# A two-layer decoder: the first two groups become single pairs of batches, the second a few steps behind the first

## The chip, the cores and the metric

The kernel runs on one core of a Trainium2 chip. The metric is the device time of one execution in microseconds. The core has five engines that run side by side, each working through its own queue in order: TensorE (PE, matrix products and transposes, with a separate row PEld for loading its stationary operand), VectorE (DVE), ScalarE (ACT), GpSimd (POOL) and SyncE (SP), which here issues all DMA transfers.

## The reference

Two decoder layers over 32 batches of 56 tokens with 128 features. Every batch has a memory of 1500 rows (`ctx_1024`). All of it is float32. Cut to what matters:

```python
x = LN(x + L0_attn(x))        # 16 heads of 8, window of 32
x = LN(x + L0_xattn(ctx, x))  # one head of 128 over 1500 memory rows
x = LN(x + L0_ffn(x))         # 8 experts of 512 (gelu), top 2
x = LN(x + L1_attn(x))        # gated recurrent mixer: tanh projections and a scan over tokens
x = LN(x + L1_xattn(x, ctx))  # 16 heads of 64 over 1500 memory rows
x = LN(x + L1_ffn(x))         # 1 shared + 8 routed experts of 256 (silu), top 2
```

The experts are computed densely: every token goes through every expert, and the mixing weights are zero for all but two. So an expert's weights are loaded once for each group of tokens that passes.

## The kernel before

**Groups.** The 32 batches form 16 pairs of two (112 tokens, `TP`) and 8 groups of two pairs (224 tokens, `T`). For a group there are three kinds of work:

- `pre`: self-attention, cross attention of layer 0, its experts, the recurrent mixer, and the queries for the cross attention of layer 1, folded with the keys' weights (`m1`). The cross attention of layer 0 also transposes each batch's memory and stores it in HBM as `memT`.
- `attention`: the cross attention of layer 1, with 896 query rows (16 heads of 56 tokens) against 1500 memory rows for each batch. It runs batch by batch in two blocks of 512 and 384 query rows. `load_attended` (L1050) brings a batch's memory into `amN`, `load_attended_T` (L1053) its transposed form into `amT`. The scores lie in two large buffers with the tags `s512` and `s384`.
- `post`: the output projection and the experts of layer 1.

**Order of the work.** Each kind of work is a Python generator, and a `Thread` steps it from one `yield` to the next. A `yield` gives the time that the thread should stay away, in a count of modelled TensorE time. The main loop steps `attention` and, after each step, the `pre` of the next group and the `post` of the last one, as far as they are due: `pre` is spread so that it ends at 88% of its group's attention, with `PRE_US` = 74 and `POST_US` = 31 as their modelled sizes. The order in which instructions are written down is a priority: a scheduler at build time places them in the engines' queues when it reckons their inputs and buffers are there, so that DMA loads with nothing to wait for go out far ahead of their place in the code.

**The opening.** Before the first score of `attention` there has to be a first group with its queries. The kernel opens with groups 0 and 1 together, four pairs:

```python
starts = [Thread(opening_a(0)), Thread(opening_a(1), aside)]
...
together(*starts, folding, lag=10)
load_attended_T(0)
together(Thread(opening_b()))
together(Thread(opening_c(0)), Thread(opening_c(1), aside))
```

`opening_a` is the self-attention and the cross attention of one group, each with its two pairs one after the other; `opening_b` sends both groups through the experts of layer 0 on one load of the weights; `opening_c` is the mixer, and for group 0 the queries. Group 1 uses other places than group 0 (`aside`): it keeps its tiles inside the buffers that attention uses later (`s512`, `s384`, the query buffer `qo[2]`, a tile `m`), reads memory into `amN` instead of `cxN`, and takes its PSUM banks from the pool `p_s` (three banks, tag `s`) instead of `p_f` (two banks, tag `f`). In the profile its tiles bear these names: `s<-qo,wu` is group 1's `f<-xT,wu`. `folding` multiplies the head weights of layer 1 (`in_heads_dram`) into `m1` and `n1`. `together` steps its threads in turn.

**Lines to know.** L142 and L151 are the helpers for every matmul and every transpose, so these are told apart by tiles. `load_x0` (L481) loads the memory of a pair, two DMAs. L507 stores `memT`. L642 and L644 load an expert's `wu` and `wd` (256 KB each, four buffers). L681 is the gelu, L705 adds an expert's output to `acc`. L809 copies queries into `qo`, of which there are three, one for a pair. L345 is the last step of a normalization. L998 copies scores out of PSUM.

Of the kernel before, what the change touches and what calls it, by code (L numbers as in the profile page):

```python
# [15 lines left out]
G = 4  # L16
NG = B // G
T = G * S
NJ = G // 2
TP = 2 * S  # L20
H0, DH0, WIN = 16, 8, 32
# [38 lines left out]
PRE_US, POST_US = 74.0, 31.0  # L60
# [4 lines left out]
def decoder_kernel(  # L65
# [232 lines left out]
    def wide_tile(tag, bufs=1):  # L298
        return work.tile([P, T], F32, tag=tag, name=tag, bufs=bufs)

# [61 lines left out]
    def ahead(a, b, tag="res"):  # L362
        r = tok_tile(tag)
        nc.gpsimd.tensor_tensor(r, a, b, ALU.add)
        return r
# [12 lines left out]
    def self_attention(xs):  # L378
        xT = to_features(xs, "xT")
        res = [ahead(t, obias) for t in xs]  # L380
        yield HOP
        qT, kT, oT = wide_tile("qT0"), wide_tile("kT0"), wide_tile("oT0")
        affine(qT, linear(sqw("wq0"), xT, T), vcol("bq0"))
        yield 0
        affine(kT, linear(sqw("wk0"), xT, T), vcol("bk0"))
        yield 0
        vs, kbs = [], []
        for j in range(NJ):
# [21 lines left out]
        for j in range(NJ):  # L410
# [59 lines left out]
        for j in range(NJ):  # L470
            ys.append(normalize(plus(linear(pair(oT, j), sqw("wo0"), D, TP), res[j]), "y"))
            yield 0
# [4 lines left out]
    def load_x0(p, g):  # L477
        cxN = contexts_0()
        for i in range(2):
            b = g * G + 2 * p + i  # L480
            nc.sync.dma_start(cxN[i][:, :, :D], mem[b].rearrange("(p c) d -> p c d", p=PK))  # L481

    def cross_attention_0(xs, g):
        cxN, qpad = contexts_0(), here(qpad0, "qpad")
# [3 lines left out]
        qp, oT, vT = wide_tile("qT0"), wide_tile("oT0"), wide_tile("kT0")  # L488
        affine(qp, linear(sqw("xq0"), xT, T), vcol("xbq0"))
# [3 lines left out]
            linear(sqw("xk0"), qp, T).rearrange("p (b s) -> p b s", b=G),  # L493
# [3 lines left out]
        for p in range(NJ):  # L497
            cxT = [big_tile(i) for i in range(2)]
            for i in range(2):
# [7 lines left out]
                nc.sync.dma_start(memT[g * G + 2 * p + i], cxT[i][:, : CK * PK])  # L507
# [48 lines left out]
            if p + 1 < NJ:  # L556
                load_x0(p + 1, g)
            elif g == 1:
                load_attended(0)
            elif max(g + 1, 2) < NG:  # L560
                load_x0(0, max(g + 1, 2))
# [7 lines left out]
            yield LOAD if p + 1 < NJ else HOP  # L569
        affine(vT, linear(sqw("xv0"), oT, T), vcol("xbv0"))  # L570
        yield HOP
        ys = []
        for j in range(NJ):
            ys.append(normalize(plus(linear(pair(vT, j), sqw("xo0"), D, TP), res[j]), "y"))
            yield 0
# [60 lines left out]
    def experts_0(groups):  # L636

# [9 lines left out]
        def each():  # L647
            for k in range(len(groups)):
                place["aside"] = aside if k else None
                yield k  # L650
            place["aside"] = None

        ws = weights(0)
        xT, w, acc, hT = {}, {}, {}, {}
        for k in each():
            xT[k] = to_features(groups[k], "xT")
        yield HOP
        for k in each():
            lg = tiny.tile([TP, NJ, E], F32, tag="lg", name="lg", bufs=2)
            nc.vector.tensor_copy(lg, router(xT[k], C_R0))  # L660
            picks = top2(lg)
            p1 = tiny.tile([TP, NJ], F32, tag="p1", name="p1", bufs=2)
            p2 = tiny.tile([TP, NJ], F32, tag="p2", name="p2", bufs=2)
            nc.vector.tensor_tensor(p2, picks[1][0], picks[0][0], ALU.subtract)
            nc.scalar.activation(p2, p2, AF.Exp)
            nc.vector.tensor_scalar_add(p1, p2, 1.0)
            nc.vector.reciprocal(p1, p1)
            nc.vector.tensor_tensor(p2, p2, p1, ALU.mult)
            w[k] = mix(picks, (p1, p2))
        yield 0  # L670
        for e in range(E + 1):
            last = (ws, dict(hT))
            if e < E:
                if e > 0:
                    ws = nxt
                if e + 1 < E:
                    nxt = weights(e + 1)
                for k in each():
                    hT[k] = hidden_tile()
                    for u in range(nu):  # L680
                        nc.scalar.activation(  # L681
                            hT[k][:, u, :],
                            linear(ws[0][:, u * D : (u + 1) * D], xT[k], T), AF.Gelu,
                            bias=vec[:, C_BUP + e * nu + u : C_BUP + e * nu + u + 1],
                        )
                        if len(groups) == 1:
                            yield 0
                yield 0
            for k in each():
                if e == 0:  # L690

                    wT = work.tile([E, T], F32, tag="wT", name="wT", bufs=1)
                    ps = bank(p_f, "f")
                    for j in range(NJ):
                        mm(pair(ps[:E], j), w[k][:, j, :], ident[:TP, :TP])
                    nc.vector.tensor_copy(wT, ps[:E, :T])
                    if len(groups) == 1:
                        yield HOP
                    acc[k] = [
                        plus(linear(pair(wT, j), bdn, D, TP), groups[k][j], "acc")  # L700
                        for j in range(NJ)
                    ]
                else:
                    for j in range(NJ):
                        nc.vector.scalar_tensor_tensor(  # L705
                            acc[k][j], down(last[1][k], last[0][1], nu, j),
                            w[k][:, j, e - 1 : e], acc[k][j], ALU.mult, ALU.add,
                        )
                        if len(groups) == 1:
                            yield 0  # L710
        both = []
        for k in each():
            both.append([normalize_twice(a, "y") for a in acc[k]])
        yield NORM
        return both


    def recurrent_mixer(both):
        hp = here(hp0, "hp")
        res, hs = [], [h for _, h in both]  # L720
        for t, _ in both:
            r = tok_tile("res")
            nc.vector.scalar_tensor_tensor(r, t, 2.0, rowb("bout1"), ALU.mult, ALU.add)
            res.append(r)
        affine(
            hp[:, :, 1 : S + 1], transposed(hs).rearrange("p (b s) -> p b s", b=G),
            vcol("lnb1"), vcol("lng1"),
        )
        mT = wide_tile("xT")
        m3 = mT.rearrange("p (b s) -> p b s", b=G)  # L730
# [11 lines left out]
        def state_in(c0, scale, bias, i):  # L742
            t = small[:, i * T : (i + 1) * T]
            nc.scalar.activation(
                t, linear(sq[:, c0 : c0 + SD], mT, T, SD), AF.Tanh, bias=bias[:, i : i + 1],
# [10 lines left out]
        u, g = wide_tile("kT0"), wide_tile("qT0")  # L756
        nc.scalar.activation(u, linear(sqw("wi1"), mT, T), AF.Tanh, bias=vcol("bi1"))

        new = small[:, 3 * T : 4 * T]
# [4 lines left out]
        nc.vector.memset(dec.rearrange("p (b s) -> p b s", b=G)[:, :, 0:1], 0.0)  # L764
# [4 lines left out]
        nc.scalar.activation(g, linear(sqw("wg1"), mT, T), AF.Tanh, bias=hbg, scale=0.5)  # L769
        yield 2.5  # L770

        z = wide_tile("oT0")
        nc.vector.scalar_tensor_tensor(
            z, linear(hwso, sta, T), vcol("bso1"), u, ALU.add, ALU.subtract
# [5 lines left out]
        for j in range(NJ):  # L780
# [10 lines left out]
    def query_input(both, g):  # L791
        res1[g] = [ahead(t, gbias, f"res1{g % 2}") for t, _ in both]
        hs = [h for _, h in both]
        xT = wide_tile("xT")
# [3 lines left out]
    def queries_1(xT, g):  # L798
        while not projected(2 * g - 2):
            yield None  # L800
        for i in range(H1 // 2):
            ps = bank(p_f, "f")
            for k in range(2):
                mm(ps[:, k * T : (k + 1) * T], m1[:, 2 * i + k, :], xT)
            src = ps[:, : 2 * T].rearrange("p (h b s) -> p b h s", h=2, b=G)
            for j in range(NJ):
                dst = qo[(2 * g + j) % 3][:, :, 2 * i * S : (2 * i + 2) * S]
# [89 lines left out]
    def load_x(g):  # L897
        xs = []
        for j in range(NJ):
            t = tok_tile("xin", 4)  # L900
            nc.sync.dma_start(t, x[g * T + j * TP : g * T + (j + 1) * TP, :])
            xs.append(t)
# [3 lines left out]

    def pre(g):
        if g == 1:
            yield from queries_1(query_input(both.pop(1), 1), 1)
            return  # L910
        xs = xin.pop(g) if g in xin else load_x(g)
# [4 lines left out]
        (xs,) = yield from experts_0([xs])  # L916
        xs = yield from recurrent_mixer(xs)
        xT = query_input(xs, g)
        yield HOP
        yield from queries_1(xT, g)  # L920


    first, both = {}, {}

    def opening_a(g):
        xs = load_x(g)
        load_x0(0, g)
        yield 0
        xs = yield from self_attention(xs)
        first[g] = yield from cross_attention_0(xs, g)  # L930

    def opening_b():
        both[0], both[1] = yield from experts_0([first[0], first[1]])

    def opening_c(g):
        both[g] = yield from recurrent_mixer(both[g])
        if g == 0:
            xT = query_input(both.pop(0), 0)
            yield HOP
            yield from queries_1(xT, 0)  # L940
# [3 lines left out]
    def post(g):  # L944
        xs, t0 = [], g * T
        for j in range(NJ):
            pp = 2 * g + j
# [4 lines left out]
            for h in range(H1):  # L952
# [12 lines left out]
                r, ps[:TP, :D], tgate[:TP], res1[g][j], ALU.mult, ALU.add  # L965
# [333 lines left out]
```

## Time and profile before

| | us |
|---|---|
| median of three runs | 2382.88 |
| lowest and highest | 2378.03, 2383.84 |
| the profiled execution | 2383.31 |
| its span, first to last instruction | 2381.6 |
| PE busy | 2247.1 (94%) |
| DVE busy | 1427.0 (60%) |
| ACT busy | 1262.7 (53%) |
| POOL busy | 254.3 (11%) |

The page gives busy times of each engine over the span and in 40 slices of it, in tenths. A timeline row has the start, the duration, the engine, the line, the operation and what it writes and reads (`out<-in`), a count where like instructions are merged, and in brackets the idle time ahead of it with what ended it. A float32 matmul shows as two instructions. Matmuls are pipelined, so that the distance from start to start, the pitch, tells what they cost in a dense stretch, and the mean duration does not. `PEclk` is the share of full speed that TensorE's clock was granted.

### The profile page before, as it was taken

The numbers are of one execution on the slowest core, as the hardware profiler recorded it, in microseconds if no ns is written. First come the engines' busy times: TensorE is split into PE (matmuls) and PEld (weight loads), VectorE is DVE, ScalarE is ACT, GpSimd is POOL, SyncE is SP. The second block draws the span as 40 slices with busy tenths as digits, with TensorE's granted clock in tenths as the row PEclk, the third lists the DMA queues.
The fourth block names the chain that finished last, engine by engine and source line by source line (L and its number), as shares of the span: only waits on it lengthen the run. The fifth ranks groups of instructions, "written<-read, shape, count | busy, mean of one in ns | idle before, by whom it ended". The sixth has DMA issues, their size and how long they took to land. (4 is left out here: it accounts for less than half of the span.)

```text
span 2381.6 us, 37426 instructions
## 1 busy us (share of the span) xinstructions
PE 2247.1 (94%) x14906; PEld 1769.6 (74%) x14906; DVE 1427.0 (60%) x2755; ACT 1262.7 (53%) x2212; POOL 254.3 (11%) x416
## 2 busy tenths in 40 slices
PE   6769799999999999999999999999999999999997
PEld 4548477767876779767887787777787678878787
DVE  3422566766576664766557665666647665566664
ACT  1324365555655456555565556554655555655542
POOL 3100200110021000220003100220002200020000
PEclk8878899999999999999999999999999999999998
DMA  5233010114320233113221133201331022210212
GB/s 157 79 113 91 11 40 26 29 54 122 93 66 16 66 102 108 47 29 108 85 82 37 53 103 94 72 27 59 111 97 58 27 91 62 71 42 28 80 34 82
DMA packets 158159, 163.81 MB, mean 69 GB/s; under 512 B 7417, under 2 KB 134817, under 8 KB 157857
## 3 DMA queue, kind: packets, MB, share of 16 engines
q1 hardware_dynamic: 157984, 161.42, 22.1%
q8 instruction: 118, 1.93, 0.3%
q14 instruction: 57, 0.46, 0.1%
HBM read 135.90 MB, written 25.49 MB: 68 GB/s over the span
## 5 line engine op out<-in xcount | busy, mean ns | idle before, releaser
L142 PE MATMUL v<-amN,s 125*128 125x129 f32 x5376 | 701.3, 276 | 1.8 <-ACT s L1086 1.8
L142 PEld LDWEIGHTS v<-amN,s 125*128 125x128 f32 x5376 | 663.2, 192 | 45.9 <-issue 29.7
L142 PE MATMUL s<-qo,amT 128*125 128x512 f32 (+1 forms) x1536 | 651.5, 547 | 4.7 <-ACT s L998 4.4
L998 ACT COPY s<-s 125x512 f32<-125x512 f32 (+1 forms) x768 | 396.6, 538 | 188.2 <-PE s L142 186.9
L1083 DVE TENSOR_TENSOR s<-s,nb 125x1536 f32<-125x1536 f32 (+1 forms) x256 | 394.3, 1557 | 108.9 <-ACT nb L1075 108.8
L142 PEld LDWEIGHTS s<-qo,amT 128*125 128x125 f32 x1536 | 264.0, 188 | 190.5 <-issue 114.9
L1086 ACT ACTIVATE s<-s 125x1536 f32<-125x1536 f32 (+1 forms) x256 | 337.6, 1327 | 91.3 <-DVE s L1083 87.1
L1001 DVE TENSOR_TENSOR m<-m,s 125x1024 f32<-125x1024 f32 (+1 forms) x256 | 279.0, 1090 | 70.4 <-ACT s L998 65.7
L342 POOL TENSOR_SCALAR rs<-mv 112x1 f32<-112x1 f32 x116 | 46.0, 396 | 1797.9 <-DVE mv L336 1598.8
L1103 ACT ACTIVATE ao<-v,rz 128x128 f32<-128x128 f32 x224 | 80.2, 361 | 176.7 <-DVE rz L1101 174.3
L681 ACT ACTIVATE hT<-f,vec 128x224 f32<-128x224 f32 x224 | 95.3, 449 | 96.8 <-PE f L142 95.1
L142 PE MATMUL f<-xT,wu 128*128 128x224 f32 x448 | 124.2, 381 | 2.8 <-DMA wu<-in_wup_dram 2.0
L142 PE MATMUL f<-pxT,w 128*128 128x224 f32 (+1 forms) x576 | 118.2, 343 | 2.1 <-DMA w<-in_gate_dram 1.3
L1001 DVE TENSOR_TENSOR m<-s 125x1024 f32<-125x1024 f32 x64 | 69.7, 1090 | 83.5 <-ACT s L998 83.2
L142 PEld LDWEIGHTS f<-wd,hT 128*112 128x112 f32 x896 | 104.7, 178 | 13.4 <-ACT hT L681 5.1
L705 DVE SCALAR_TENSOR_TENSOR acc<-f,wmix,acc 112x128 f32<-112x128 f32 x112 | 39.2, 350 | 125.8 <-PE f L142 125.8
L142 PE MATMUL f<-wd,hT 128*112 128x128 f32 x896 | 113.3, 275 | 0.0
L1075 ACT COPY nb<-t 125x512 f32<-125x512 f32 x64 | 34.0, 532 | 148.3 <-PE t L142 148.1
L142 PEld LDWEIGHTS f<-pxT,w 128*128 128x128 f32 x576 | 99.4, 195 | 15.3 <-issue 3.2
L142 PEld LDWEIGHTS f<-xT,wu 128*128 128x128 f32 x448 | 74.0, 194 | 21.2 <-ACT hT L681 7.4
L142 PEld LDWEIGHTS f<-w,h 128*112 128x112 f32 x512 | 67.6, 178 | 24.0 <-issue 9.2
L142 PE MATMUL f<-w,h 128*112 128x128 f32 x512 | 79.7, 279 | 2.0 <-DVE th L870 1.9
(313 smaller groups left out, 2694.2 us busy)
## 6 DMA issues: line engine op xcount, KB each, us to landing
amN<-in_mem_dram SPq DMA_DIRECT2D x36, 750.0 KB
amT<-memT SPq DMA_DIRECT2D x32, 750.0 KB, 4.4
cxN<-in_mem_dram SPq DMA_DIRECT2D x28, 750.0 KB
memT<-big SPq DMA_DIRECT2D x28, 750.0 KB, 5.0
wu<-in_wup_dram SPq DMA_DIRECT2D x56, 256.0 KB, 2.8
wd<-in_wdn_dram SPq DMA_DIRECT2D x56, 256.0 KB, 2.7
w<-in_gate_dram SPq DMA_DIRECT2D x72, 128.0 KB, 2.3
w<-in_up_dram SPq DMA_DIRECT2D x72, 128.0 KB, 2.5
```

The source lines that it names most:

```text
L142: nc.tensor.matmul(ps, lhsT=lhsT, rhs=rhs, start=start, stop=stop)
L342: nc.gpsimd.tensor_scalar(rs, mv[:, 1:2], mul, add, ALU.mult, ALU.add)
L681: nc.scalar.activation(hT[k][:, u, :], linear(ws[0][:, u * D : (u + 1) * D], xT[k], T), AF.Gelu, bias=vec[:, C_BUP + e * nu + u : C_BUP + ...
L705: nc.vector.scalar_tensor_tensor(acc[k][j], down(last[1][k], last[0][1], nu, j), w[k][:, j, e - 1 : e], acc[k][j], ALU.mult, ALU.add,)
L998: nc.scalar.copy(s[:, c, :], ps[:PK, :n])
L1001: nc.vector.tensor_tensor(m, a, s[:, c - 1 : c + 1, :], ALU.max)
L1075: nc.scalar.copy(nb, ps[:PK, :n])
L1083: nc.vector.tensor_tensor(c, c, nb.unsqueeze(1).to_broadcast([PK, 3, n]), ALU.add)
L1086: nc.scalar.activation(c, c, AF.Exp)
L1103: nc.scalar.activation(o, po[:, :D], AF.Copy, scale=rz)
```

## The change

The groups get different sizes: pair 0 alone, pair 1 alone, and then seven groups of two pairs.

- The helpers of `pre` take the number of pairs from their input. `experts_0` works on one group and returns `acc` before its normalization.
- `opening(0)`, the leader, goes from the self-attention to the queries with pair 0. `opening(1)`, the follower, starts six steps later with pair 1 in the places aside. It waits for the leader to have written down all its experts, goes through the experts with its own loads of the weights, and copies its `acc` out of the places aside by GpSimd once the leader is through. The head folding starts at step 12.
- The mixer and the queries of pair 1 are now `pre(1)`, stepped beside attention without a limit; then comes the `pre` of pairs 2 and 3, spread over the attention of pairs 0 and 1, and so on. There are now seven `pre` of two pairs beside attention; there were six.
- `load_x0` for pair 2 and `load_x` for its group are written down after the opening. `load_attended(0)` follows the follower's cross attention, `load_attended_T(0)` the leader's.
- The main loop paces by the attention time over all pairs (`PAIR_US` = 82.7) instead of from the start of each group; `post` keeps its pairs and its pacing. A `yield NORM` is added in the mixer.

```diff
-G = 4
-NG = B // G
...
+GROUPS = [[0], [1]] + [[p, p + 1] for p in range(2, NPAIR, 2)]
+NG = len(GROUPS)
...
     def pre(g):
         if g == 1:
-            yield from queries_1(query_input(both.pop(1), 1), 1)
+            yield from behind_experts(early.pop("acc"), 1)
             return
...
-    def opening_a(g):
+    def opening(g):
         xs = load_x(g)
-        load_x0(0, g)
+        load_x0(GROUPS[g][0])
         yield 0
         xs = yield from self_attention(xs)
-        first[g] = yield from cross_attention_0(xs, g)
...
+        xs = yield from cross_attention_0(xs, g)
         if g == 0:
...
+            load_attended_T(0)
+            acc = yield from experts_0(xs)
+            early["weights"] = True
+            yield from behind_experts(acc, g)
+            return
+        load_attended(0)
+        while "weights" not in early:
+            yield None
+        acc = yield from experts_0(xs)
+
+        while not leader.over:
+            yield None
+        place["aside"] = None
+        early["acc"] = []
+        for a in acc:
+            t = tok_tile("acc")
+            nc.gpsimd.tensor_copy(t, a)
+            early["acc"].append(t)
...
-    together(*starts, folding, lag=10)
-    load_attended_T(0)
-    together(Thread(opening_b()))
-    together(Thread(opening_c(0)), Thread(opening_c(1), aside))
+    n = 0
+    while not (leader.over and follower.over):
+        for t, at in ((leader, 0), (folding, 12), (follower, 6)):
+            if n >= at and not t.over:
+                t.step()
+        n += 1
+    load_x0(GROUPS[2][0])
+    xin[2] = load_x(2)
...
+        at = main.spent / PAIR_US
+        g = next((g for g in range(1, NG) if not pres[g].over), None)
+        if g == 1:
+            until(pres[1], 1e9)
+        elif g is not None:
+            since = 0 if g == 2 else GROUPS[g - 1][0]
+            part = (at - since) / (GROUPS[g][0] - since)
+            until(pres[g], PRE_US * part / 0.88)
```

## The prediction

> **What bounds the kernel now.** I read the page's slices first, then the span cut into stages, then the timelines of TensorE and of SP's queue. The page:
>
> ```profile
> PE   6769799999999999999999999999999999999997
> ...
> PEclk8878899999999999999999999999999999999998
> ```
>
> Of forty slices of 59.5 us, only the first five (and the last) are not full. The same, cut where the work changes:
>
> ```profile
> 8.00:77.00 69.00, 53.82 (x437) 38.28 (x438) 30.42 (x53) 17.97 (x36) 20.53 (x27) 0.80 0.39 119
> 77.00:113.00 36.00, 27.98 (x213) 21.13 (x213) 14.42 (x39) 14.44 (x28) 4.78 (x12) 0.86 0.30 111
> 113.00:145.00 32.00, 13.90 (x50) 8.94 (x51) 2.31 (x4) 3.67 (x7) 0.00 (x0) 0.60 0.46 140
> 145.00:174.00 29.00, 22.00 (x164) 15.82 (x162) 11.91 (x33) 11.70 (x21) 2.54 (x8) 0.85 0.24 85
> 174.00:200.00 26.00, 23.15 (x90) 17.73 (x91) 8.22 (x50) 9.70 (x20) 0.42 (x1) 0.61 0.43 114
> 200.00:241.00 41.00, 41.00 (x301) 39.54 (x301) 8.69 (x25) 18.76 (x48) 0.00 (x0) 1.00 0.24 73
> 241.00:276.20 35.20, 19.77 (x84) 13.66 (x83) 20.52 (x73) 7.24 (x18) 14.61 (x38) 0.71 0.05 14
> 276.20:435.60 159.40, 156.65 (x890) 116.99 (x889) 103.12 (x120) 99.41 (x165) 0.00 (x0) 1.00 0.10 30
> 435.60:2113.10 1677.50, 1634.22 (x11047) 1286.28 (x11047) 1058.74 (x2024) 954.72 (x1655) 196.94 (x286) 0.99 0.23 70
> 2113.10:2381.60 268.50, 253.88 (x1643) 210.77 (x1642) 168.32 (x336) 123.57 (x215) 9.24 (x16) 0.98 0.18 53
> ```
>
> Columns: stretch, length, then busy PE, PEld, DVE, ACT, POOL, granted clock, DMA share, GB/s. From 276.2 us, where the first score matmul of the big attention starts, PE is busy 97 to 98% at clock 1.00: there every matmul costs its pitch, and nothing else counts. The 276.2 us ahead of it are latency and DMA, with a clock down to 0.60. So a piece of work is dear in the opening and cheap behind it. The change moves work across this border.
>
> What one pair of batches waits for in the opening stands in SP's queue:
>
> ```profile
> 28.48 8.00 SPq L1165 DMA_DIRECT2D s<-in_heads_dram  x1
> ...
> 109.53 7.02 SPq L481 DMA_DIRECT2D cxN<-in_mem_dram  x2
> 116.64 15.40 SPq L481 DMA_DIRECT2D amN<-in_mem_dram  x2
> ...
> 163.50 6.81 SPq L481 DMA_DIRECT2D cxN<-in_mem_dram  x2
> 170.41 16.28 SPq L1050 DMA_DIRECT2D amN<-in_mem_dram  x2
> 186.79 7.95 SPq L642 DMA_DIRECT2D wu<-in_wup_dram  x1
> ```
>
> Four loads of a batch's memory take 34 us (109.5 to the last one's first use at 143.7, at about 100 GB/s), and PE stands for them in 113 to 145. At 163.5 the same four loads go out again for later work, and the expert weights wu queue behind them: issued at 186.79, in use at 199.79.
>
> **The change, part by part.** Let X be the moment of the first score matmul, 276.2 now. The sum is X, plus 2105.4 (2381.6 - 276.2), plus what moves behind X.
>
> *Work that moves behind X.* Pairs 2 and 3 lose their joint opening and become an ordinary `pre`. Its price: groups 1 to 6 take 1677.5 / 6 = 279.6 us each, made of attention, one `pre` and one `post`. Attention alone shows between two reloads of amT in the first group:
>
> ```profile
> 298.03 0.33 SPq L1053 DMA_DIRECT2D amT<-memT  x1
> ...
> 343.53 0.34 SPq L1053 DMA_DIRECT2D amT<-memT  x1
> ...
> 385.01 0.34 SPq L1053 DMA_DIRECT2D amT<-memT  x1
> ```
>
> It is 41.5 us (nothing beside it) to 45.5 us (with some queries) a batch, 43 taken: 172 for four. 107.6 remain for `pre` and `post`; the kernel's own weights 74 : 31 split them into 75.8 and 31.8. Bounds: 41.5 gives 80, 45.5 gives 69; I take 76. Window 0 had no `pre` and now has one, as windows 1 to 6 do; DVE 63% and ACT 57% busy there leave them room, so PE's pitch is the price. Its DMAs go along: four memory loads, four stores of memT and sixteen loads of weights lift the DMA share of window 0 from 0.10 to the 0.23 of the others, which hides them there.
>
> *Pair 1* now does its mixer and queries beside attention. Queries: 32 matmul instructions of 112 columns. Their pitch, from this row (32 in 3.56 us to the next start):
>
> ```profile
> 495.63 3.72 PE L142 MATMUL f<-qo,n 128*128 128x112 f32 x32
> 499.19 1.07 PE L142 MATMUL v<-amN,s 125*128 125x129 f32 x8
> ```
>
> 0.111 us each, 3.6 us; some 20 more for the mixer at 0.11, 2 us. Out goes what window 0 did for group 1: 32 of 224 columns at 0.19, 6.1 us. Net -0.5. The mixer's long chain (241 to 269 in the trace) hides under attention, which needs pair 1 only a pair later; uncovered it would cost its 28 us. The extra `yield NORM` and the new pacing are emission only: each `pre` still has to be through at 88% of its window, 0. The GpSimd copy of acc is one of 0.5 us, and attention's first score tile waits for it, since the follower's work lies in the buffers s512 and s384.
>
> *X, stage by stage.* (1) Self-attention: the first pair's oT is written at 52.64, the second's at 75.44; the second goes, and with it one of two normalizations: xT of the cross attention comes at 83.07 now, about 57 then (52.6 + 4.7 for one tile, reading the same chain). The wait for `heads1`, in use at 45.85, stays: PE takes it in order. (2) The first cross pair runs from 83.07 until cxN is free at 109.53, 26.4 us, with both groups in step. The leader is six steps ahead, which I count as 4 us: cxN free at 57 + 26.4 - 4 = 80 (75 if the head folding lies behind the leader's chain, 84 if it gets nothing from its lead). (3) The second cross pair, its four loads and the wait (113 to 167) go. (4) The experts. The loads at L481 for the next group and at L1050 for batches 0 and 1 are free to go out at 80, ahead of wu of expert 2, whose buffer is only freed by expert 0. If they do, as at 163.5, the distance 163.50 to 199.79 = 36.3 us repeats: expert 2 starts at 116. (5) From there 6 experts of the leader and 8 of the follower, each set streaming its 4 MB of weights anew, 16 passes instead of 8. The pass now, for four pairs:
>
> ```profile
> 199.79 0.99 PE L142 MATMUL f<-xT,wu 128*128 128x224 f32 x4 [2.01 <-DMA wu<-in_wup_dram]
> ...
> 206.49 0.92 PE L142 MATMUL f<-xT,wu 128*128 128x224 f32 x4
> ```
>
> 6.65 us, all PE. For one pair PE needs 8 x 0.111 + 8 x 0.109 = 1.8 us, so PE no longer bounds it. Two other loops do. Two banks serve two 224-column products in 1.21 us (199.79 to 201.00), so four ups take up to 2.4 and four downs 0.9: 3.3, less for 112 columns. And wu goes out about one pass ahead of its use and lands 2.7 us after issue, with a 0.34 us issue of wd ahead of it: 3.0. I take 3.1; 14 x 3.1 = 43.4. (6) Last down, copy, first score: 3. X = 80 + 36.3 + 43.4 + 3 = 163.
>
> *A rule against it.* Row first: the clock is 1.00 in 200 to 241, where PE is dense, and 0.61 to 0.71 on both sides. The Trainium skill, "TensorE: Matmul & The Clock Gate", section "A second HAM failure mode: psum-queue depth-cycling", says that small idle gaps between groups of matmuls that cycle through banks make the clock swing between half and full. A pass with 1.8 us of PE work in 3.1 is such a pattern. By the rule the work takes 3.5, with some of the eviction waits on top 4.3: X = 180. The first cross attention, just as full of gaps, got 0.86, which lies nearer to full; I keep 3.1 and put the rule in the range.
>
> **Sum.** 163 + 2105.4 + 75.5 = 2343.9, against 2381.6: -37.7. The profiled execution took 2383.3, 1.7 over its span and 0.4 over the median 2382.9. So 2346.
>
> **Rivals.**
> A (0.55): as above, 2346.
> B (0.25): the scheduler puts wu ahead of the four memory loads. For it: those serve nobody before attention. Against: at 163.5 they went first. Expert 0 starts at 88, 16 passes of 3.1 follow: X = 88 + 49.6 + 3 = 141, time 2324.
> C (0.08), slower: weight streaming becomes the wall. Each pass fetches 512 KB for half as many tokens as any pass before. If a pass still takes 6.65 us (wu and wd landing one after the other, 2 x 2.7 and their issues, behind other traffic), X = 116 + 14 x 6.65 + 3 = 212 and time 2395. It decides from 5.8 us a pass (X = 201). Against it: 2.7 us of landing overlaps the pass before.
> D (0.12): little of it arrives: the leader gains nothing from its lead (84) and the clock stays half (4.3): X = 84 + 36 + 60 + 3 = 183, time 2366. That the change doesn't do what it says would also end here: if the in-order queues make the leader wait for the follower at each step, the lead is worth nothing.
>
> **How the numbers follow.** About 0.3%, 7 us, is what a measurement of this kernel tells from no change (the three runs spread 0.24%). A, B and most of D lie under 2376: faster 0.87; D's upper end and C's lower end, 0.05; C's rest 0.08. The range takes B with a pass of 2.8 us (X = 136) and D with a `pre` of 80: 2318 to 2370; above it lie C and a tail of D, below it a faster B.
>
> **What would show it.** In the changed profile: first score matmul near 163; four in_mem loads in SP's queue just ahead of the third wu (A) or behind it (B); a pass of the experts of about 3.1 us in the spacing of wu, clock above 0.8 there; the first window about 76 us longer than its 159; windows after it unchanged at 279 to 280 us each. Wrong would be a first score matmul behind 200, passes of 5.8 us or more, or a first window that grows by more than 85.

## The result: 2445 us, 2.6% slower

The changed kernel takes 2445.4 us (median of 5 runs, 2443.1 to 2447.7), the kernel before 2383.1 in the same job: a ratio of 1.0264, with a 95% interval of 1.0249 to 1.0279. The profiled execution has a span of 2444.0 us. The forecast was 2346, with a range of 2318 to 2370: wrong in sign. The windows behind the first were to stay at 279 to 280 us; the five in the middle took 291 each.

The opening did what it was meant to. TensorE's busy tenths in the page's slices, after the change:

```profile
PE   5789999998999999998999989999899999999998
```

TensorE is full from the fourth slice on, where before it was full from the sixth. But before, every slice from there to the last but one was a 9; now 8s are strewn along the row. A slice is 61 us and the loss a few per cent in many of them: its size shows only when the span is cut where the work changes. Stretch, length, busy PE, PEld, DVE, ACT, POOL, granted clock, DMA share, GB/s, after the change:

```profile
45.50:89.70 44.20, 43.48 (x287) 32.18 (x287) 17.33 (x34) 14.42 (x28) 2.41 (x6) 0.73 0.39 135
89.70:125.70 36.00, 16.23 (x105) 12.02 (x103) 8.56 (x38) 9.61 (x19) 1.48 (x4) 0.64 0.40 106
125.70:150.00 24.30, 19.67 (x120) 16.32 (x121) 6.68 (x32) 11.57 (x31) 1.44 (x4) 0.90 0.47 149
...
175.60:715.50 539.90, 505.40 (x3358) 388.90 (x3356) 325.24 (x593) 310.69 (x528) 59.59 (x90) 0.98 0.22 67
715.50:2171.30 1455.80, 1380.59 (x9232) 1092.98 (x9231) 886.49 (x1691) 842.87 (x1415) 153.74 (x240) 0.98 0.22 67
2171.30:2444.00 272.70, 256.01 (x1652) 210.14 (x1650) 173.53 (x355) 126.63 (x221) 14.45 (x24) 0.98 0.18 52
```

The marks are the first score matmul (175.60) and the reloads of amT for batches 8 (715.50) and 28 (2171.30) in SP's queue. The same two stretches of the kernel before, between the same events:

```profile
276.20:710.40 434.20, 424.78 (x2705) 326.81 (x2704) 277.89 (x453) 256.57 (x435) 32.30 (x48) 1.00 0.19 57
710.40:2113.10 1402.70, 1366.08 (x9232) 1076.46 (x9232) 883.98 (x1691) 797.56 (x1386) 164.65 (x238) 1.00 0.23 70
```

| stretch | before | forecast | after | after - forecast |
|---|---|---|---|---|
| to the first score matmul (X) | 276.2 | 163 | 175.6 | +12.6 |
| from there to batch 8 | 434.2 | 509.7 | 539.9 | +30.2 |
| batches 8 to 28, five windows | 1402.7 | 1402.7 | 1455.8 | +53.1 |
| batch 28 to the end | 268.5 | 268.5 | 272.7 | +4.2 |
| span | 2381.6 | 2343.9 | 2444.0 | +100.1 |

(The forecast for the second row is 434.2 plus the moved 75.5.) The largest loss is in the five windows that the change was supposed to leave alone. They hold the same 9232 TensorE instructions in both kernels. What TensorE waits for in them, first after, then before (total us, times, longest):

```profile
PE f L145 <- DMA w<-in_gate_dram: 25.9, 8, 4.0
PE f L154 <- DVE h L348: 12.0, 5, 2.4
PE f L145 <- ACT big L525: 10.2, 6, 2.6
```

```profile
PE f L151 <- ACT big L447: 11.8, 5, 2.4
PE f L151 <- DVE h L345: 6.9, 5, 1.4
```

All rows of that view sum to 73.4 us after and 35.4 before, so 38 of the 53 us are waits. The other 15 are in the busy column, 1366 to 1381 us for the same matmuls at a clock of 0.98 instead of 1.00: the longer waits go with a lower clock. The new first row says what is new: the weights of post's gate arrive late. SP's queue in one window shows why (start, duration of the issue, transfer), first after:

```profile
1127.20 6.95 SPq L485 DMA_DIRECT2D cxN<-in_mem_dram  x2
1134.24 7.38 SPq L817 DMA_DIRECT2D w<-in_gate_dram  x1
...
1142.66 0.78 SPq L1051 DMA_DIRECT2D amN<-in_mem_dram  x1
1143.55 7.43 SPq L817 DMA_DIRECT2D w<-in_gate_dram  x1
```

```profile
1146.01 3.33 PE L145 MATMUL f<-pxT,w 128*128 128x224 f32 x8 [3.87 <-DMA w<-in_gate_dram]
```

The like place in the kernel before:

```profile
1094.99 6.87 SPq L481 DMA_DIRECT2D cxN<-in_mem_dram  x2
1110.91 0.74 SPq L1050 DMA_DIRECT2D amN<-in_mem_dram  x1
1118.53 2.88 SPq L507 DMA_DIRECT2D memT<-big  x2
1126.19 0.33 SPq L828 DMA_DIRECT2D w<-in_gate_dram  x1
...
1143.21 7.55 SPq L828 DMA_DIRECT2D w<-in_gate_dram  x1
```

A gate weight is 128 KB and its issue takes 0.33 us when the queue is free. Behind the two cxN loads (750 KB each) it takes 7.38, behind amN 7.43, and TensorE stands for it. A held issue is not new in itself: the kernel before has one of 7.55 at 1143.21, and no wait of TensorE for a gate weight in its rows. What is new is that the weight is needed before it has come. What the change rewrites in these windows is the main loop, which decides when each step of `pre` and `post` is written beside attention, and two pauses in `pre`: a `NORM` more, and one for each expert less. So the question for the runs was whether that loop is the cause, and how an order turns into time.

### The profile page after: what moved, and what is told of

Same layout as the page of the kernel before. It is cut to its first block, busy times and chain, and to the rows that moved or that the text cites. A ratio compares the mean times of both kernels' runs of the same rounds, so it can differ in the third digit from the quotient of the medians.

```text
span 2444.0 us, 37877 instructions
## 1 busy us (share of the span) xinstructions
PE 2262.9 (93%) x15024; PEld 1783.3 (73%) x15024; DVE 1440.3 (59%) x2798; ACT 1335.6 (55%) x2293; POOL 250.6 (10%) x416
## 5 line engine op out<-in xcount | busy, mean ns | idle before, releaser
L145 PE MATMUL v<-amN,s 125*128 125x129 f32 x5376 | 720.3, 280 | 4.7 <-ACT s L1087 3.0
L145 PEld LDWEIGHTS v<-amN,s 125*128 125x128 f32 x5376 | 674.9, 195 | 52.0 <-issue 35.6
L145 PE MATMUL s<-qo,amT 128*125 128x512 f32 (+1 forms) x1536 | 642.3, 543 | 9.7 <-ACT s L999 9.0
L145 PE MATMUL f<-pxT,w 128*128 128x224 f32 (+1 forms) x576 | 131.2, 370 | 40.3 <-DMA w<-in_gate_dram 31.6
L676 ACT ACTIVATE hT<-f,vec 128x224 f32<-128x224 f32 (+1 forms) x256 | 103.8, 437 | 113.3 <-PE f L145 111.7
L145 PE MATMUL f<-xT,wu 128*128 128x224 f32 (+1 forms) x512 | 130.7, 359 | 20.1 <-DMA wu<-in_wup_dram 17.2
L145 PE MATMUL f<-wd,hT 128*112 128x128 f32 x960 | 124.2, 278 | 1.5 <-DVE acc L693 0.9
L145 PEld LDWEIGHTS f<-xT,wu 128*128 128x128 f32 x512 | 85.4, 194 | 44.1 <-issue 23.8
L858 ACT ACTIVATE th<-f 128x448 f32<-128x448 f32 (+1 forms) x81 | 40.6, 501 | 111.3 <-PE f L145 108.6
L436 POOL TENSOR_TENSOR big<-big,mx 112x448 f32<-112x448 f32 x60 | 72.8, 1234 | 151.0 <-PE f L145 130.6
```

The lines of the kernel that those rows point to most:

```text
L145: nc.tensor.matmul(ps, lhsT=lhsT, rhs=rhs, start=start, stop=stop)
L436: nc.gpsimd.tensor_tensor(s3[:, c, :], s3[:, c, :], mx[:, c].unsqueeze(2).to_broadcast([TP, 4, TP]), ALU.subtract,)
L676: nc.scalar.activation(hT[:, u, :], linear(ws[0][:, u * D : (u + 1) * D], xT, nt), AF.Gelu, bias=vec[:, C_BUP + e * nu + u : C_BUP + e * n ...
L858: nc.scalar.activation(th, pg[:, : nu * n], AF.Tanh, scale=0.5)
```

## The experiments

Of the main loop two rules are new. First, `pre` is paced by `at`, counted from zero in units of 82.7 us of the kernel's own modelled TensorE time. When attention asks for the queries of pair 2, `at` is 1.887 and not 2, because the values of the last blocks are still to come; each `pre` therefore starts 0.113 x 82.7 = 9.3 of these units late in a window of 165. A second NORM pause comes on top. Second, `post` has a head start of 4 and runs on a line that is late by as much. The lateness is in the written order, and these figures are those of the kernel's own model; no trace shows them. What it costs is what the runs measure. Each run is given with its ratio to the kernel before in its own job.

**Pre back on time, in the changed kernel.** Three kernels: pace reset at each window, one NORM pause removed, both.

```
-            part = (at - since) / (GROUPS[g][0] - since)
+            part = (main.spent - began) / (2 * PAIR_US)   # began: reset at each window
...
         acc = yield from experts_0(xs)
-        yield NORM
```

> The changed kernel with one edit: a pre is paced from the moment its window starts, as before the change, and no longer from the absolute count of attention time, which at the start of a window still lacks 9.3 units of values. Theory L (each window got 10 us longer because pre starts late and, with one more pause, its queries are all forced out at the end of the window with attention held): the start moves back by 9.3 units, the extra pause of 6 stays, so most of the 10 us a window goes: windows of 280 to 284 us, time 2370 to 2395. Rival M (the windows are longer because of what moved: seven pre with their loads colliding with the expert weights of post): windows stay at 290, time 2440 to 2450.

> The changed kernel with one edit: of the two pauses of 6 units between the experts and the mixer of a pre only one is left, as before the change. Theory L: the queries come 6 units sooner, the late start of 9.3 stays; about half of the loss goes: windows of 283 to 288 us, time 2395 to 2430. Rival M: no change, 2440 to 2450.

> The changed kernel with both edits: pre paced from its window's start, and one pause only. Theory L: windows as before the change, 279 to 281 us; with the first score at about 180 us as in the changed kernel, 180 + 2105 + 76 + 2 = 2363, so 2355 to 2375. Rival M: 2440 to 2450.

Measured: reset 2437.5 (1.0237, 1.0222 to 1.0252), one pause 2447.9 (1.0281, 1.0262 to 1.0300), both 2422.9 (1.0172, 1.0157 to 1.0187). With both, the five windows take 1440.8 of after's 1455.8. All three are misses for the simple form of the theory: putting pre right gives back some 20 us, not all; the pause alone gives nothing, as rival M had it.

**Pre made late, in the kernel before.**

```
-            work_.append((pres[group + 1], PRE_US, p / 0.88))
+            work_.append((pres[group + 1], PRE_US, (p - 9.3 / share) / 0.88))
...
+        if len(groups) == 1:
+            yield NORM
```

> The kernel before the change with both faults put in: pre paced 9.3 units late in every window and a second pause of 6 units between experts and mixer; its opening and its groups stay. Theory L: six windows 10 us longer each, time 2435 to 2450. Rival M: no change, 2378 to 2390.

Measured: 2463.2 (1.0348, 1.0330 to 1.0365), 82 us over the kernel before. Nothing else of the change is in this kernel. A late pre (lag and pause together) alone is enough to make more than the whole loss. With the three runs ahead of it, it says that the second rule must matter too.

**The whole old loop in the changed kernel, and the new post rule alone in the kernel before.**

```
# changed kernel (one yield NORM goes as well)
-        at = main.spent / PAIR_US
...
+        p = (main.spent - began) / 165.0
...
+            until(pres[window + 2], PRE_US * max(p, 0.0) / 0.88)
+        if window > 0:
+            until(posts[window - 1], POST_US * p / 0.85)
+        if window >= 0:
+            until(posts[window], 4.0 * p)
...
# kernel before
-            work_.append((posts[k], POST_US, p / 0.85 if k < group else -1.0))
+            lead = p - (9.3 / share if k < group else 0.0)
+            work_.append((posts[k], 1.0, 4.0 + POST_US * lead / 0.85 if k < group else -1.0))
...
-            work_.append((posts[group], 4.0, p))
+            if p > 0.5 and (group == 0 or posts[group - 1].over):
+                work_.append((posts[group], 4.0, 1.0))
```

> The changed kernel, with the main loop of before put back (both the pre and the post of a window paced from the attention time spent since the window's first score matmul) and a single NORM pause. Theory P (all of the loss is pacing: the first half in the pre, shown by the kernel before made late, the rest in the post): windows of 279 to 281 us, first score matmul still near 176, so 176 + 2105 + 75.5 + 2 = about 2358, ratio 0.990. Theory R (what the reset of the pre left over, 7.4 us a window, lies in other code: the dropped pause per expert, the buffers, the loads): windows of 286 to 288, about 2418, ratio 1.015.

> The kernel before, with the changed kernel's rule for post alone (4 us of head start ahead of the straight line, which itself runs 9.3/165 late; the next post opened only when the one ahead of it is over and half of the window is past); the pre stays as before. Theory P: this rule costs about what is left over in the changed kernel after its pre was put right, some 7 us a window: about 2381 + 6 x 7 = 2425, ratio 1.018. Theory R (the rest lies in other code): no change, 2379 to 2387. A third way: the two rules only hurt together, then 2387 to 2400.

Measured: the changed kernel with the old loop takes 2380.7 us (0.9995, 0.9983 to 1.0007), and its five windows take 1403.2 us, as before to half a microsecond. That settles the place of the 53 us: it is the loop, since with the second pause put back (below) the windows are 1406.8. The time itself missed the expected 2358, because two other terms are still too long: in the profiled execution X is 181.2 and the stretch to batch 8 takes 535.3. That execution (2389.8) is the slowest of twelve and 9 us over their median, so a part of these two terms may be chance; the other kernels with this opening have X at 174 to 178. The new post rule alone costs the kernel before 28 us (2408.9; 1.0110, 1.0095 to 1.0125), its windows 1423.1.

**The fourth corner: late pre with the old post rule.**

```
-            until(pres[window + 2], PRE_US * max(p, 0.0) / 0.88)
+            until(pres[window + 2], PRE_US * max(p - 9.3 / 165.0 * (window > 0), 0.0) / 0.88)
...
         acc = yield from experts_0(xs)
+        yield NORM
```

> As the old-loop kernel, but pre is again late as in the changed kernel (9.3 of 165 late from the second window on, and the second NORM pause); post keeps the rule of before. Together with the changed kernel (both rules new, 2445), the one with pre put right alone (2423) and the old-loop kernel (2381) this fills a table of two by two. If the two costs add: 2381 + 22 = about 2403, windows of 284. If late pre costs as much with the old post rule as it did in the kernel before (13.7 us a window there): about 2460, windows of 293 to 294, and the new post rule would be a partial remedy for a late pre.

Measured: 2465.7 (1.0363, 1.0345 to 1.0381), slower than the changed kernel itself. The five windows, in us:

| | old post rule | new post rule |
|---|---|---|
| pre on time | 1403.2 | 1440.8 |
| pre late | 1471.1 | 1455.8 |

The two rules don't add. With pre on time the new post rule costs 38; with a late pre it saves 15. That is why repairing pre alone gave so little.

**Which part of the lateness, and is there a cliff?** Three more on the old-loop kernel: the second pause alone, the lag of 9.3 alone, and half the lag (4.6).

> As the old-loop kernel, with the second NORM pause in pre alone. By the written order (TensorE time of the kernel's own model) pre is through at every need of attention, as in the old-loop kernel. Theory K (a cliff: only what of pre is not yet written when attention needs it costs, since it is then written in one lump ahead of the next score matmul): no change, 2373 to 2388, windows of 280 to 281. Theory G (every pause and every delay squeezes the later steps and costs in proportion): about a third of the 85 us between this kernel and the one with late pre and old posts, 2400 to 2415.

> As the old-loop kernel, pre 9.3 of 165 late from the second window on, a single NORM pause. In the written order 2.4 us of the 73.5 of each pre (three of its eight query steps) are still to come at the need; with the second pause 6.3 (all eight). Theory K: 2.4/6.3 of 85 us, about 2413, windows of 285 to 287. Theory G: two thirds or more of the 85, 2437 or above.

> As the old-loop kernel, pre 4.6 of 165 late from the second window on, a single NORM pause. In the written order nothing of pre is left at the need. Theory K: no change, 2373 to 2388, windows of 280 to 281. Theory G: half of what 9.3 costs, 2405 to 2425.

Measured: pause alone 2388.3 (1.0029, 1.0018 to 1.0039), half the lag 2441.3 (1.0251, 1.0227 to 1.0276), the whole lag 2488.8 (1.0451, 1.0431 to 1.0471). The cliff falls: half the lag costs about 60 us though by the written order nothing of pre is left over at the need, and the kernel with less left over (2.4, whole lag) is slower than the one with all eight query steps left (6.3, whole lag and pause). The lag carries the loss, about 9 us a window for 4.6 and 17 for 9.3; the pause alone costs next to nothing, and on top of the lag it even takes some 20 us off (2465.7 against 2488.8, in two jobs; 15 in the five windows); why is open. The trace of the late-only kernel shows a part of what lateness does. Line 525 is the copy of cross-attention scores into `big`, the buffer from which memT is being stored. What ScalarE was idle for ahead of that line, in the five windows, in the late-only kernel and then in the old-loop kernel (us, times):

```profile
DMA memT<-big: 43.8, 5
```

```profile
DMA memT<-big: 12.5, 6
```

In the kernel before it is 9.0, in the changed kernel 21.9, with half the lag 34.1. One of the five, in SP's queue and on TensorE:

```profile
1149.96 7.50 SPq L1050 DMA_DIRECT2D amN<-in_mem_dram  x1
1157.56 7.88 SPq L817 DMA_DIRECT2D w<-in_gate_dram  x1
...
1166.97 0.84 SPq L512 DMA_DIRECT2D memT<-big  x2
```

```profile
1175.45 1.94 PE L145 MATMUL f<-big,qpad 128*64 128x500 f32 x4 [7.97 <-ACT big L525]
```

The stores stand behind amN, a gate weight and amT; the copy waits for the stores, everything behind the copy in ScalarE's order waits with it, and TensorE stands 8 us. All such waits of TensorE for line 525 sum to 37.2 us in the late-only kernel's windows and 3.2 in the old-loop kernel's. The place in the queue is only a part of the wait. The issue starts 2.8 us after the last copy into `big` (1164.2), and the first copy of scores comes another 7 us after the issue, at 1174.82. In these microseconds the DMA engines are full (last two columns: DMA share, GB/s). The load of amT was issued just ahead of the stores (1166.49), where the old-loop kernel issues it some 10 us behind them (1134.85 after 1125.10):

```profile
1166.00:1175.00 9.00, 1.48 (x9) 0.52 (x4) 2.19 (x2) 0.18 (x1) 0.00 (x0) 0.71 0.98 312
```

**Is the queue the cause, or a bystander?** The same late-only kernel with the cxN loads on POOL's queue, then with the memT stores there; and the changed kernel as it is with both.

```
-            nc.sync.dma_start(cxN[i][:, :, :D], ...)
+            nc.gpsimd.dma_start(cxN[i][:, :, :D], ...)
...
-                nc.sync.dma_start(memT[...], ...)
+                nc.gpsimd.dma_start(memT[...], ...)
```

> The late-only kernel (2489), with the loads of cxN issued on POOL's queue instead of SP's. Theory Q (lateness costs because pre's large transfers fall into SP's queue beside post's weights and attention's amT and amN, so that each waits for the others' issue: in the late-only kernel ScalarE stands 43.8 us in five windows for the memT store behind them, 12.5 in the old-loop kernel): SP's queue is relieved of two issues of 7 us a pair, windows fall from 297 to 285 to 290, time to 2425 to 2455. Theory S (lateness costs in itself: pre's chain is squeezed and attention waits for its queries; the queue is a bystander): within 8 us of 2489.

> The late-only kernel (2489), with the stores of memT issued on POOL's queue instead of SP's. Theory Q: the store no longer waits behind amN, w and amT in SP's queue, ScalarE's wait for it at the line of the score copy falls from 43.8 us to about 12, and 30 to 45 us come off: 2444 to 2459. Theory S: within 8 us of 2489, with the wait gone to something else. If POOL's queue itself is held by its own waits, slower.

> The changed kernel as it is (2445), with both moved to POOL's queue: the loads of cxN and the stores of memT. Theory Q: a good part of the 53 us that its five steady windows are longer than before comes back: windows from 291 to 282 to 286, 2405 to 2425. Theory S: 2437 to 2453.

Measured: late with the loads moved 2457.4 (1.0320, 1.0300 to 1.0340), late with the stores moved 2453.8 (1.0290, 1.0269 to 1.0312), the changed kernel with both 2399.9 (1.0071, 1.0045 to 1.0097). So the queue on which a transfer is issued is a cause: one word in each of two lines takes 45 us off the changed kernel without touching its pacing. Its five windows fall to 1429.9, 26 less. Of these 17 are waits: the 25.9 us for gate weights are gone, and other waits rise by 9. The other 9 are busy time (1380.6 to 1372.1). At the place shown above, the gate weight that stood behind cxN is now issued at once; the next still stands behind amN, and TensorE no longer waits for it:

```profile
1099.60 0.35 SPq L817 DMA_DIRECT2D w<-in_gate_dram  x1
...
1104.89 0.78 SPq L1051 DMA_DIRECT2D amN<-in_mem_dram  x1
1112.65 8.74 SPq L817 DMA_DIRECT2D w<-in_gate_dram  x1
```

Another 14 come off X (161.2), where the cxN loads no longer stand ahead of wu, and 10 off the stretch to batch 8 (530.1). In the late-only kernel the two moves take 15 and 21 us out of windows that are 83 too long (1471.2 and 1465.6 of 1486.2), less than I expected. ScalarE's wait for the stores was to fall from 43.8 us to about 12 once they were moved. It fell less:

```profile
DMA memT<-big: 31.7, 10
```

TensorE's waits for line 525 fall from 37.2 to 15.2 there, but a store that is issued at once still needs 5.6 us (1152.17 to 1157.77) beside amT. So in the late-only kernel the queue explains a fifth and a quarter by the two moves; they weren't run together, and what the rest is made of stays open. The candidates are transfers that now meet in the DMA engines and the squeezed chain of pre; no run took them apart. Nor is the order in the queue the only thing that the moves change: on POOL's queue the cxN loads go as packets of 1.25 KB on average instead of 0.5 KB (11,232 packets for 14.06 MB in the windows of the late-only kernel with these loads moved), and no run separates the two.

**The opening: who has to wait for wu?** In the changed kernel TensorE stands 16.5 us for the third wu. Two kernels on the old loop: all four memory loads held back until the leader's experts are done, or three of them until the follower's are (amN of batch 0 stays early).

The second one's edit:

```
+    def held(tiles, acc):          # a one-column copy that the load has to wait for
+        for t in tiles:
+            nc.vector.tensor_copy(t[:TP, 0, 0:1], acc[:, 0:1])
...
+        held((amN[1], *cxN), early["acc"][0])
```

> As the old-loop kernel, and in the opening the four memory loads that serve nobody yet (two into cxN, two into amN) are held until the leader's last expert is computed, so that the weights wu of expert 2 go out ahead of them. If the 16.5 us wait of TensorE for wu at 109 to 126 is what the opening loses there: first score matmul 14 to 17 us earlier, near 160, and 14 to 17 us less in all than the old-loop kernel. If the passes of the follower are held by something else (its own accumulators, the eviction), or the held loads are then late for the first values of attention: first score matmul at 170 or later, or a new wait of attention for amN, and less than 5 us gained.

> As the old-loop kernel, with three of the four memory loads (both of cxN, and amN of batch 1) held until the follower's experts are computed; amN of batch 0 stays where it is. Theory H (the loads are in the way of the weights wherever they fall among the 16 passes, so they belong behind them): no wait of TensorE for wu above 5 us, first score matmul at 165 to 170 (181 in the old-loop kernel), about 13 us less in all: 2364 to 2370, ratio 0.993 to 0.995. Rival (the passes are paced by weights alone, so the time shows up again as short waits for wu): first score matmul at 176 or later, less than 5 us gained. Second rival: cxN or amN of batch 1 is late in the first window, and the gain goes there.

Measured: all four behind the leader's 2390.2 (1.0035, 1.0024 to 1.0047); three behind the follower's 2363.6 (0.9932, 0.9913 to 0.9951). In the first the loads merely fell among the follower's passes, and the wait moved there:

```profile
176.67 2.02 PE L145 MATMUL s<-m,wu 128*128 128x112 f32 x8 [13.40 <-DMA wu<-in_wup_dram]
```

In the second, whose profiled execution is the fastest of four, no such wait is left, and attention starts at

```profile
159.20 8.75 PE L145 MATMUL s<-qo,amT 128*125 128x512 f32 x20
```

**The stretch to batch 8.** The old-loop kernel with pair 1's mixer and queries done in the opening.

```
     pres[0].over = True
+    while not pres[1].over:
+        pres[1].step()
```

> As the old-loop kernel, with pair 1's mixer and queries done in the opening, behind the follower's experts, instead of beside the first window's attention. In the old-loop kernel the first score matmul is 313 us ahead of the reload of amT for batch 5, against 219 before: 95 us more where one pre was priced at 75.5. Theory M (pair 1's chain, squeezed in ahead of group 2's pre, makes the extra 19): the distance falls by 15 to 20, to about 296, and the first score matmul comes 15 to 28 us later; in all 0 to +10 against the old-loop kernel. Theory N (the pre of group 2 itself is dear in a window that has no post to go with it): the distance falls by no more than 6, the first score matmul comes later all the same, in all +12 to +25.

Measured: 2377.7 (0.9989, 0.9979 to 1.0000). The distance that the theories were put to, from the first score matmul to the reload for batch 5, falls by 1 us only (313.4 to 312.2), which speaks for N. To batch 8 the stretch falls from 535.3 to 527.9. That is not shown to be pair 1's doing: the old-loop kernel with the second pause leaves pair 1 beside attention and takes 527.6 there, and the medians of the two, each against the kernel before in its own job, differ by 1 us. So some 18 of the 26 us by which the stretch was over the forecast lie in group 2's pre and what goes beside it; the others are within what kernels with the old loop and pair 1 beside attention differ by (527.6 to 535.3). Both theories expected X to come later; it did not: 176.2, against 175.6 in the changed kernel.

**The best of it, and the same hold in the kernel before.**

> The hold-late kernel with pair 1's mixer and queries done in the opening as well. In the mixer-open kernel that took 7 us of waits out of the first two windows, and its first score matmul (176) was no later than in the changed kernel, because the chain ran beside the follower's passes. If this adds to the held loads: 2356 to 2361. Rival: now that TensorE no longer stands for wu, the chain has less to hide behind and moves the first score matmul from 159 to 170 or later: 2364 to 2372.

> The kernel before, with the same three memory loads (cxN for group 2, amN of batch 1) held until its experts are computed. In its trace wu of expert 2 was issued at 186.8 behind them and in use at 199.8, with TensorE idle for much of 174 to 200. Theory Q (the held loads are worth the same in either opening, so that the new grouping itself is worth nothing): 12 to 18 us less than before, 2363 to 2369, level with the hold-late kernel. Rival (the loads hurt the changed kernel more, since it streams the weights twice): 0 to 6 us less than before, and the hold-late kernel stays ahead by over 10.

Measured: old loop, held loads and mixer in the opening 2362.0 (0.9922, 0.9907 to 0.9936); the kernel before with the held loads 2374.1 (0.9970, 0.9959 to 0.9981). The first is the fastest kernel of this study, level with the one with held loads alone (their intervals overlap). Each against the kernel before in its own job, the hold is worth about 15 us in the new opening and 6 in the old. With its pacing and its loads repaired, the new grouping is 10 to 12 us better than the old one with the same hold.

## Why the prediction was wrong, step by step

**The step that failed in sign**: "The extra `yield NORM` and the new pacing are emission only: each `pre` still has to be through at 88% of its window, 0." The first half is true, and the conclusion doesn't follow. When a step is written decides its place in in-order queues, and its transfers stand in SP's queue with those of attention and `post`. The old loop put back into the changed kernel takes the five windows from 1455.8 to 1403.2; that is the price of this zero, 53 us, with the tail's 4.2 on top (268.4 with the old loop). Nor was pre through at 88%: the line of `at` starts 9.3 units behind the need. That was to be read in the diff. I had read the 0.88, and not where its zero lies. The prediction followed the transfers through SP's queue in the opening only; for the windows it had a mean DMA share of 0.23, "which hides them there". That share hardly moved (0.23 before, 0.22 after): what changed is what stands ahead of what.

**The moved work, 76 less 0.5**: mechanism right, size wrong. The matmuls of pre in the stretch to batch 8, taken as the pitch to the next start and sorted by their tiles, rose from 78.7 us before to 153.5 with the mixer in the opening: 75. But the stretch grew by 94 there, and by 101 in the old-loop kernel. TensorE's waits in it, summed over the waits view, are 8.3 us before, 19.8 and 27.3 in these two, and 34.2 after. "DVE 63% and ACT 57% busy there leave them room" is an average and says nothing of single waits. So a pre of 76 that costs about 94 to 101 in this stretch is the mis-sized term. Whether the net of -0.5 for pair 1 was wrong too, no run shows. A slip in the sum is small: the profiled execution lay 0.4 us over the median, which was to be taken off and not added, 2345 instead of 2346.

**X, 163**: the parts, against the trace of after.
- xT of the cross attention at 57: it comes at 55.68. Right, and so is the wait for the heads, in use at 45.52.
- From there to cxN free, 22.4: it took 34.0, to 89.71. The prediction took a row in which both groups went in step and subtracted a lead of 4. In 45.50 to 89.70 TensorE is busy 43.48 of 44.20 us at a clock of 0.73: the head folding and the follower fill it, so a lead buys nothing. Rival D had half of this.
- Loads ahead of wu, 36.3: it is 36.0 (89.71 to 125.67). Right, for the reason given:

```profile
89.71 7.01 SPq L485 DMA_DIRECT2D cxN<-in_mem_dram  x2
97.42 14.81 SPq L1051 DMA_DIRECT2D amN<-in_mem_dram  x2
112.33 7.95 SPq L645 DMA_DIRECT2D wu<-in_wup_dram  x1
```

```profile
125.67 0.74 PE L145 MATMUL f<-xT,wu 128*128 128x112 f32 x2 [16.54 <-DMA wu<-in_wup_dram]
```

- Fourteen passes and the end, 46.4: 49.9. A little slow; rival C (5.8 us and more) has nothing for it.

The clock bears on this row, but the rule of the Trainium skill does not decide it. In this profile the granted clock in the leader's passes is 0.90 (125.70 to 150.00), nearer to full, as the prediction chose. The old-loop kernel issues the same matmuls in the same order there. From the third wu to the first score matmul it shows this, beside the kernel with late pre and old posts:

```profile
128.50:181.20 52.70, 47.17 (x287) 40.62 (x288) 17.07 (x65) 23.19 (x66) 3.35 (x9) 0.83 0.42 134
```

```profile
125.80:175.70 49.90, 43.60 (x286) 37.36 (x287) 17.07 (x65) 22.77 (x66) 3.34 (x9) 0.91 0.41 141
```

So at 0.83 the passes take 2.7 us longer than at 0.91; the other 2.8 us between the two X (181.2 and 175.7) were there when the third wu came into use (128.54 and 125.78). "TensorE: Matmul & The Clock Gate", section "A second HAM failure mode: psum-queue depth-cycling", was read as 4.3 us a pass, 60 for the fourteen and X = 180. The page reports it of one bf16 kernel; in eight profiles of this opening the same passes took 48 to 53 us.

**The rivals.** All of them stood in the opening, where the one decided for the slower side never came near its threshold. None let the steady windows grow, though the diff rewrites the loop that makes them, and seven windows multiply every microsecond. The 0.08 for "slower" was the chance of another mechanism.

## What to carry to other kernels

A change of pacing or of written order is not free because it adds no instruction: follow each transfer of the shifted step through its queue, and ask what small, urgent issue comes to stand behind a large one. Multiply by the number of windows; here five windows lost 53 us, and the opening's X was 13 off. Where a load serves nobody yet, put it behind the last urgent stream and not merely later: held halfway, it only moved the wait.

## What the hardware showed that was not expected

- A queue is held by large loads out of proportion to the urgent issue. The gate weight's issue takes 0.33 us alone and 7.4 to 7.9 behind memory loads.
- Longer waits came with a lower clock. In the late-only kernel the five windows are 83 us longer than in the old-loop kernel: TensorE's waits rise from 34.6 to 91.7, and the same 9.2 thousand matmuls are busy 1391 us instead of 1367, at a mean clock of 0.97 instead of 0.99.
- ScalarE's table loads, at 1.283 us each, were a suspect, since the changed kernel has 80 in the five windows and the kernel before 50. They don't go with the time: 40 with pre on time and the new post rule (1440.8 us), 50 in the old-loop kernel (1403.2) and in the late-only one (1486.2).
